# A graph layer and a small feed-forward layer: cell products in halves of a step, with a tile's product between them

## The chip, the cores and the metric

The kernel runs on one core of one Trainium2 chip. The metric is the time of one execution on the device in microseconds (us). The engines are TensorE (PE, whose weight loads the profile shows apart as PEld), VectorE (DVE), ScalarE (ACT), GpSimd (POOL) and SyncE (SP, which here only issues DMAs).

## What is computed

Inputs are `x` (8192 x 512), 131072 edges `(src, dst, edge_weight)`, a 512 x 512 weight and the weights of a seven-layer network of width 160. Cut to what matters:

```python
h   = layernorm(x) @ gnn_weight.T                     # 8192 x 512
x1  = x + segment_sum(edge_weight[:, None] * h[dst], src, 8192)
out = x1 + ffn(layernorm(x1))                         # ffn reads and writes a few columns of each row
```

For each edge a row of `h` (512 float32 numbers, 2 KB) has to be fetched by `dst`, scaled, and added to row `src`. The edges come in no order, so the kernel sorts them on the chip by the block of 128 rows that `src` lies in. There are 64 such blocks.

## The kernel before

**Heads.** The generator `project` makes `h` block by block (layer norm, transposes at L213, products at L238) and writes it to memory. Beside it the first part of the sort runs: `order(0)`.

**Sort.** `order` works on chunks of edges. A chunk (`chunk`, L328) compares the edges' blocks with the block numbers (DVE, L334), counts places with 8 products into `p_base` (L342) and 8 into `p_rank` (L357), and then puts each edge's packed address and weight into its cell by one-hot products into `p_c` (L402). These are the *cell products*. A chunk has four *quarters* (`c0` = 0, 2, 4, 6; in the code a loop in steps of SUB = 2), and each quarter has 16 values of `k` with 2 products each: 32 products. A quarter needs two operands, `blocks` (ACT, L375) and `put` (DVE, L376 and twice L384). They are made by `prepare`, which is called two quarters ahead, right behind the products of a quarter, and writes into the buffers that this quarter has just read (two buffers each). At the chunk's end ACT copies `p_c` out (L407). Seven chunks are in the first part and nine in the second. After its chunks each part runs `squeeze`, a long row of DVE operations.

**Gathered tiles.** A tile is 128 edges of one block. POOL fetches their rows with one indirect DMA (L570, 256 KB). DVE makes a one-hot matrix `hot` with the weights (L583, 28 tiles ahead). PE multiplies the two into the block's sum `p_g` (L881). Four tiles share a buffer `g`, and there are six such buffers, so POOL can be up to 24 tiles ahead of PE; a small product at L877 leads each buffer. `begin` goes through the 384 tiles of the first part, `evenly` through the 704 of the second, there with the feed-forward layers between.

**What sets the order.** PE, DVE, ACT and SP run in the order in which the program is written. The sort is a chain of generators. `chunk` yields `(tiles, blocks)`: how many gathered tiles, or head blocks, are to pass before its next step. The first part runs beside `project` and goes by `blocks`. Of the second part, `order(1)` with `fine` = 1, the first 24 steps run beside `project`, which takes them to just ahead of the first cell products; 16 more steps run straight behind it (L614), which is the rest of its first chunk and 6 steps into its second; and what is left, some eight chunks, runs beside the gathered tiles of `begin`, one step whenever the tile number `t` reaches `due` (L907). `due` grows by what each step yields; for a chunk that is 33 tiles in all. In `begin` the cell products of the four quarters stand behind tiles 0, 4, 8 and 9 of this part of a chunk.

In the profile one product of float32 is two MATMULs and two weight loads. A quarter therefore shows as 64 MATMULs of L402, a gathered tile as 2 of L881.

Of the kernel before, what the change touches and what calls it, by code (L numbers as in the profile page):

```python
# [34 lines left out]
def tile_gnn_ffn(  # L35
# [35 lines left out]
    GC, GQ, CAP, SUB = 8, 8, 40, 2  # L71
# [251 lines left out]
    def cut(n, size, fine):  # L323

        parts = -(-n // size) if fine else 1
        return [slice(n * i // parts, n * (i + 1) // parts) for i in range(parts)]

    def chunk(ck, ps_c, q, col, fine):  # L328


        hot = ck.tile([P, GC, NB, GQ], BF16, name="hot")
        for cs in cut(GC, 2, fine):
            n = cs.stop - cs.start
            nc.vector.tensor_tensor(  # L334
                hot[:, cs], each.rearrange("p (o b) g -> p o b g", o=1).to_broadcast([P, n, NB, GQ]),
                blk[:, q, cs].rearrange("p c (o g) -> p c o g", o=1).to_broadcast([P, n, NB, GQ]),
                OP.is_equal)
            yield 1, cs.stop // GC

        p_base = ps_c.tile([P, NB, GQ], F32, name="p_base")  # L340
        for c in range(GC):
            nc.tensor.matmul(p_base, above, hot[:, c], start=(c == 0), stop=(c == GC - 1))  # L342
        cum = ck.tile([P, GC, NB, GQ], BF16, name="cum")
        nc.scalar.copy(cum[:, 0], p_base)  # L344
        yield 2, 0
        for c in range(1, GC):
            nc.vector.tensor_tensor(cum[:, c], cum[:, c - 1], hot[:, c - 1], OP.add)  # L347
            if c % 2:
                yield 1, 0
        for cs in cut(GC, 2, fine):  # L350
            nc.vector.tensor_tensor(cum[:, cs], cum[:, cs], hot[:, cs], OP.mult)
            yield 1, 0
        yield 0, 2
        p_rank = ps_c.tile([P, GC, NB // GC, GQ], F32, name="p_rank")
        nb = NB // GC
        for i in range(GC):
            nc.tensor.matmul(p_rank, eye, cum[:, :, i * nb : (i + 1) * nb, :], start=(i == 0),  # L357
                             stop=(i == GC - 1))
        yield 2, 0
        rank = ck.tile([P, GC, GQ], F32, name="rank")  # L360
        nc.vector.tensor_reduce(rank, p_rank.rearrange("p c b g -> p c g b"), AX.X, OP.add)
        slot = ck.tile([P, CG, 1], BF16, name="slot")
        nc.vector.tensor_tensor(slot[:, :, 0], rank.rearrange("p c g -> p (c g)"), par, OP.add)
        yield 1, 0
        at = ck.tile([P, CG, 2, HALF], BF16, name="at")
        ready = {}

        def prepare(c0):

            if c0 >= GC:  # L370
                return
            n = SUB * GQ
            cs = slice(c0 * GQ, c0 * GQ + n)
            blocks = ck.tile([P, SUB, GQ, NB], F32, name="blocks", bufs=2)
            nc.scalar.copy(blocks, hot[:, c0 : c0 + SUB].rearrange("p c b g -> p c g b"))  # L375
            nc.vector.tensor_tensor(  # L376
                at[:, cs].rearrange("p n h s -> p n (h s)"),
                lots.rearrange("p (o h) s -> p o (h s)", o=1).to_broadcast([P, n, CAP]),
                slot[:, cs].to_broadcast([P, n, CAP]), OP.is_equal)
            yield 1, 0  # L380
            put = ck.tile([P, n, 2, 2, HALF], F32, name="put", bufs=2)
            for i, val in enumerate((val_a, val_w)):
                v = val[:, q, c0 : c0 + SUB, :].rearrange("p c (g a b) -> p (c g) a b", a=1, b=1)
                nc.vector.tensor_tensor(put[:, :, :, i, :], at[:, cs],  # L384
                                        v.to_broadcast([P, n, 2, HALF]), OP.mult)
                yield 1, 0
            ready[c0] = blocks, put

        yield from prepare(0)
        yield 0, 1  # L390
        yield from prepare(SUB)
        p_c = ps_c.tile([P, GQ, 2, HALF], F32, name="p_c")
        yield 0, 1
        nc.tensor.matmul(p_c.rearrange("p g w s -> p (g w s)"), nil[:, :P], nil, start=True,
                         stop=False)
        for c0 in range(0, GC, SUB):
            blocks, put = ready.pop(c0)
            for k in range(SUB * GQ):
                c, g = divmod(k, GQ)
                last = c0 + SUB == GC and k == SUB * GQ - 1  # L400
                for h in range(2):
                    nc.tensor.matmul(p_c[h * NB : (h + 1) * NB, g], blocks[:, c, g, :], put[:, k, h],  # L402
                                     start=False, stop=last)
            yield from prepare(c0 + 2 * SUB)
            yield 1, c0 // SUB % 2 if c0 + SUB < GC else 0
        for i, cells in enumerate((cells_a, cells_w)):
            nc.scalar.copy(cells[:, col : col + GQ * HALF].rearrange("p (g s) -> p g s", s=HALF),  # L407
                           p_c[:, :, i, :])
# [128 lines left out]
    def order(part):  # L537

        qs, col, fine = (range(QA), 0, 0) if part == 0 else (range(QA, NQ), CARRY, 1)
        with tc.tile_pool(name="ck", bufs=1) as ck, \  # L540
                tc.tile_pool(name="ps_c", bufs=1, space=PSUM) as ps_c:
            for q in qs:
                for tiles, blocks in chunk(ck, ps_c, q, col, fine):
                    yield tiles * PACE[0], blocks
                col += GQ * HALF
        with tc.tile_pool(name="sq", bufs=1) as sq, \
                tc.tile_pool(name="ps_q", bufs=2, space=PSUM) as ps_q:
            for tiles, blocks in squeeze(part, sq, ps_q, fine):
                yield tiles * PACE[1], blocks
# [45 lines left out]
    LEAD, BEGUN = 2, 24  # L595
# [15 lines left out]
        if b == NB // 2:  # L611
            x_0 = load_x(0)
    assert first is None
    for n in range(BEGUN + 16):  # L614
        if n >= begun:
            next(second)
    for t in range(early, AHEAD * GS):
# [543 lines left out]
```

## Time and profile before

| | |
|---|---|
| median of 3 runs (lowest to highest) | 2087.0 us (2076.41 to 2090.85) |
| the profiled execution: its time, its span | 2088.5 us, 2086.7 us |
| mean granted TensorE clock | 0.915 |

Busy time in us by stage, from windows of the profiled execution:

| stage (us from the start) | length | PE | DVE | ACT | POOL | DMA share | clock |
|---|---|---|---|---|---|---|---|
| heads, first part of the sort (0 to 367) | 367 | 344.6 | 260.8 | 201.6 | 22.1 | 0.32 | 0.99 |
| first gathers, rest of a chunk (367 to 412) | 45 | 20.0 | 11.2 | 6.9 | 23.5 | 0.58 | 0.62 |
| tiles with eight chunks between (412 to 843) | 431 | 379.0 | 236.1 | 77.1 | 274.3 | 0.68 | 0.92 |
| tiles with the squeeze (843 to 885) | 42 | 37.3 | 41.7 | 4.5 | 34.4 | 0.70 | 1.00 |
| the rest, most of it tiles with the layers (885 to 2086.7) | 1201.7 | 971.2 | 439.5 | 99.0 | 759.4 | 0.67 | 0.90 |

Busy times are from the first start to the last end of an engine's instructions, without its gaps. A MATMUL's end is modelled, so starts are more to be trusted than ends. "Issue" in these views is time in which an engine waited for nothing that the profile shows. A granted clock below 1 means that PE was held at a lower rate for part of the stretch.

### The profile page before, as it was taken

What the parts mean: (1) busy time and instruction counts of PE and PEld (TensorE: products, weight loads), DVE (VectorE), ACT (ScalarE), POOL (GpSimd) and SP (SyncE); (2) the same over time, 40 slices, a digit from 0 to 9 for tenths busy, and PEclk for the clock granted to TensorE, in tenths of its full rate; (3) what the DMA queues carried; (4) which work ended last, traced back from release to release, by engine and by line L of the source; (5) the groups of instructions that cost most, each with busy time, mean ns of one, the idle gap of its engine ahead of it and who ended that gap; (6) DMA issues with size and microseconds to landing.
All of it is one profiled execution on the core that took longest, in us unless ns stands there. A gap on an engine that the chain in (4) does not pass through costs nothing.

```text
span 2086.7 us, 24158 instructions
## 1 busy us (share of the span) xinstructions
PE 1752.0 (84%) x9317; PEld 841.0 (40%) x9317; DVE 989.3 (47%) x2520; ACT 389.1 (19%) x521; POOL 1113.7 (53%) x1138
## 2 busy tenths in 40 slices
PE   7999989598888988874987698897988969697878
PEld 4555544344444444322332243342433334243444
DVE  6676788365455554983322324233332434234322
ACT  5565644211211111110000010100101001010111
POOL 4000000466666666787666666666666666666550
PEclk9999999699998999988998898998989989898989
DMA  5233322567676676677786667686686857757561
GB/s 174 82 102 102 102 91 87 147 198 216 207 215 205 202 229 212 204 233 232 238 273 181 189 177 262 182 268 184 182 266 181 269 173 212 224 168 245 165 180 47
DMA packets 140923, 391.37 MB, mean 188 GB/s; under 512 B 20352, under 2 KB 21376, under 8 KB 140800
## 3 DMA queue, kind: packets, MB, share of 16 engines
q0 software_dynamic: 87952, 286.45, 45.8%
q1 hardware_dynamic: 52048, 101.72, 14.3%
q8 instruction: 76, 1.25, 0.2%
q10 hardware_dynamic: 800, 1.57, 0.2%
q14 instruction: 47, 0.39, 0.1%
HBM read 339.33 MB, written 50.33 MB: 187 GB/s over the span
## 4 chain that ended last, share of the span: by engine, by line
PE 62%; issue 11%; DVE 9%; another core or an unknown queue 9%; POOL 5%; DMA 2%; ACT 1%; DVEq 0%; POOLq 0%; ACTq 0%
PE p_g L881 34%; PE p_g L238 8%; PE p_c L402 7%; POOL g L570 5%; DVE hot L583 2%; PE p_a L666 2%; PE p_a L668 2%; DMA g<-h_rows,at_dst 2%; PE p_base L342 1%; PE p_rank L357 1%; PE p_g L213 1%; PE p_j L877 1%; PE p_b L660 1%; DVE ln L714 1%
## 5 line engine op out<-in xcount | busy, mean ns | idle before, releaser
L570 POOL DMA_INDIRECT g<-h_rows,at_dst x1088 | 1091.6, 1003 | 915.9 <-issue 646.8
L881 PE MATMUL p_g<-g,hot 128*128 128x512 f32 x2176 | 1099.1, 641 | 38.5 <-issue 38.4
L881 PEld LDWEIGHTS p_g<-g,hot 128*128 128x128 f32 x2176 | 408.0, 201 | 434.0 <-issue 423.8
L583 DVE TENSOR_SCALAR hot<-lanes,at_row,at_w 128x128 f32<-128x128 f32 x1088 | 324.9, 354 | 238.2 <-remote 111.7
L238 PE MATMUL p_g<-xg,g 128*128 128x512 f32 x512 | 237.7, 608 | 2.9 <-ACT g L215 2.9
L402 PE MATMUL p_c<-put,blocks 128*64 128x40 f32 x4096 | 163.4, 235 | 72.1 <-issue 70.5
L402 PEld LDWEIGHTS p_c<-put,blocks 128*64 128x64 f32 x4096 | 145.7, 144 | 116.1 <-issue 108.3
L375 ACT CAST blocks<-hot 128x1024 f32<-128x1024 bf16 x64 | 131.2, 2077 | 255.3 <-issue 212.0
L640 DVE TENSOR_SCALAR hb<-p_b,b_b 128x128 f32<-128x128 f32 (+1 forms) x54 | 18.1, 336 | 257.1 <-PE p_b L660 93.3
L238 PEld LDWEIGHTS p_g<-xg,g 128*128 128x128 f32 x512 | 94.8, 195 | 99.9 <-issue 95.7
L877 PEld LDWEIGHTS <-hot 128*1 128x1 bf16 x272 | 21.5, 79 | 238.8 <-issue 209.3
L384 DVE TENSOR_TENSOR put<-at,val_a 128x640 f32<-128x640 bf16 x64 | 52.8, 824 | 119.1 <-remote 75.7
L347 DVE TENSOR_TENSOR cum<-cum,hot 128x512 bf16<-128x512 bf16 x112 | 47.6, 425 | 87.9 <-ACT cum L344 72.4
L877 PE MATMUL p_j<-g,hot 128*1 128x4 bf16 x272 | 45.7, 168 | 49.5 <-issue 25.3
L643 ACT ACTIVATE ha<-p_a,b_a 128x512 f32<-128x512 f32 (+1 forms) x54 | 34.6, 640 | 243.7 <-remote 103.1
L171 ACT ACTIVATE rstd_f<-mv_f,eps 128x8 f32<-128x8 f32 (+1 forms) x9 | 2.7, 300 | 395.1 <-DVE st L863 220.2
L936 DVE TENSOR_TENSOR xu<-xu,p_g 128x512 f32<-128x512 f32 x64 | 43.7, 682 | 61.1 <-PE p_g L881 23.1
L770 ACT COPY back<-p_v 128x256 f32<-128x256 f32 (+1 forms) x9 | 3.3, 371 | 358.8 <-PE p_a L652 177.1
L891 DVE TENSOR_TENSOR xg<-xg,p_g 128x512 f32<-128x512 f32 x64 | 43.6, 682 | 55.4 <-PE p_g L881 53.3
L668 PEld LDWEIGHTS p_a<-hb,w_z 128*128 128x128 f32 x360 | 49.7, 200 | 18.4 <-issue 17.9
L213 PE MATMUL p_g<-ident,g 128*128 128x128 f32 x256 | 40.3, 282 | 19.5 <-ACT g L204 13.4
L376 DVE TENSOR_TENSOR at<-lots,slot 128x640 bf16<-128x640 bf16 x64 | 52.4, 819 | 0.3
(182 smaller groups left out, 1152.0 us busy)
## 6 DMA issues: line engine op xcount, KB each, us to landing
g<-h_rows,at_dst POOLq DMA_INDIRECT x1088
xg<-in_x_dram SPq DMA_DIRECT2D x16, 1024.0 KB
x_rows<-xg SPq DMA_DIRECT2D x32, 512.0 KB
xu<-x_rows SPq DMA_DIRECT2D x16, 1024.0 KB
g<-in_x_dram SPq DMA_DIRECT2D x31, 512.0 KB
h_rows<-g SPq DMA_DIRECT2D x31, 512.0 KB
out_dram<-xu SPq DMA_DIRECT2D x7, 2048.0 KB
xg<-in_gnn_wT_dram ACTq DMA_DIRECT2D x1, 1024.0 KB
```

The source lines that it names most:

```text
L213: nc.tensor.transpose(p_t[:, k * P : (k + 1) * P], t[:, 2 + b % 2, k * P : (k + 1) * P], ident)
L238: nc.tensor.matmul(p_h, t[:, b % 2, k * P : (k + 1) * P], gw[:, k, :], start=(k == 0), stop=(k == KD - 1))
L347: nc.vector.tensor_tensor(cum[:, c], cum[:, c - 1], hot[:, c - 1], OP.add)
L375: nc.scalar.copy(blocks, hot[:, c0 : c0 + SUB].rearrange("p c b g -> p c g b"))
L376: nc.vector.tensor_tensor(at[:, cs].rearrange("p n h s -> p n (h s)"), lots.rearrange("p (o h) s -> p o (h s)", o=1).to_broadcast([P, n, C ...
L384: nc.vector.tensor_tensor(put[:, :, :, i, :], at[:, cs], v.to_broadcast([P, n, 2, HALF]), OP.mult)
L402: nc.tensor.matmul(p_c[h * NB : (h + 1) * NB, g], blocks[:, c, g, :], put[:, k, h], start=False, stop=last)
L570: nc.gpsimd.indirect_dma_start(out=g[:, k, :], out_offset=None, in_=h_rows, in_offset=bass.IndirectOffsetOnAxis(ap=at_dst[part][:, i : i + ...
L583: nc.vector.tensor_scalar(hots[n][:, k, :], lanes, at_row[part][:, i : i + 1], at_w[part][:, i : i + 1], op0=OP.is_equal, op1=OP.mult)
L668: nc.tensor.matmul(p_a[:, g, :], w_z[:, i, g, :], last_hb, start=False, stop=((g + 1) * T % 512 == 0 or g == NG - 1))
L877: nc.tensor.matmul(p_j[:, part, :], hot[:, GS - 1, :].bitcast(BF16)[:, 1:2], g.rearrange("p k d -> p (k d)").bitcast(BF16).rearrange("p (k ...
L881: nc.tensor.matmul(p_g, hot[:, i, :], g[:, i, :], start=(k == 0), stop=(k == TILES[part] - 1))
```

## The change

Where `fine` is set (the second part), `chunk` yields once more within each quarter, after 8 of its 16 values of `k`, with half a tile; the yield at the quarter's end goes from one tile to half a tile, so that a chunk's sum stays 33. The count of steps that run straight behind `project` goes from 16 to 20, since one chunk's cell products are among them and now have four more yields.

```diff
                 for h in range(2):
                     nc.tensor.matmul(p_c[h * NB : (h + 1) * NB, g], blocks[:, c, g, :], put[:, k, h],
                                      start=False, stop=last)
+                if fine and k == SUB * GQ // 2 - 1:
+                    yield 0.5, 0
             yield from prepare(c0 + 2 * SUB)
-            yield 1, c0 // SUB % 2 if c0 + SUB < GC else 0
+            yield 1 - 0.5 * fine, c0 // SUB % 2 if c0 + SUB < GC else 0
...
-    for n in range(BEGUN + 16):
+    for n in range(BEGUN + 20):
         if n >= begun:
             next(second)
```

## The prediction

> **What bounds the kernel now.** I began with the page's costliest groups, to see how much of the change's own work there is.
>
> ```profile
> L570 POOL DMA_INDIRECT g<-h_rows,at_dst x1088 | 1091.6, 1003 | 915.9 <-issue 646.8
> L881 PE MATMUL p_g<-g,hot 128*128 128x512 f32 x2176 | 1099.1, 641 | 38.5 <-issue 38.4
> L402 PE MATMUL p_c<-put,blocks 128*64 128x40 f32 x4096 | 163.4, 235 | 72.1 <-issue 70.5
> ```
>
> The cell products keep PE for 163 us and have 72 us of idle time before them that no visible wait explains. Second, the waits of the stage in which the change acts, 412 to 843 us:
>
> ```profile
> POOL g L570 <- PE p_g L881: 89.5, 25, 14.8
> PEld p_c L402 <- issue: 76.3, 112, 1.9
> ...
> PE p_c L402 <- issue: 46.8, 83, 1.7
> ```
>
> POOL waits 89.5 us in 25 pieces for a buffer that PE has not freed, so PE sets the pace here; and PE loses time to "issue" inside the cell products. Third, the timeline of PE shows where in a run of products it is lost. This is the first quarter of one chunk; columns are start, length, line, count, idle time before.
>
> ```profile
> 481.85 1.59 PE L402 MATMUL p_c<-put,blocks 128*64 128x40 f32 x46
> 483.72 0.33 PE L402 MATMUL p_c<-put,blocks 128*64 128x40 f32 x5 [0.28 <-issue]
> ...
> 486.57 0.33 PE L402 MATMUL p_c<-put,blocks 128*64 128x40 f32 x4 [1.08 <-issue]
> 487.30 0.23 PE L402 MATMUL p_c<-put,blocks 128*64 128x40 f32 x1 [0.39 <-issue]
> ...
> 503.34 2.06 PE L402 MATMUL p_c<-put,blocks 128*64 128x40 f32 x64
> 505.33 1.12 PE L881 MATMUL p_g<-g,hot 128*128 128x512 f32 x2
> 506.39 2.08 PE L402 MATMUL p_c<-put,blocks 128*64 128x40 f32 x64
> ```
>
> I call a MATMUL with its weight load a pair: a tile is 2, a quarter 64. 46 pairs run at 31 ns, and then pairs come by ones and fives at steps of 0.72 us. A full quarter at speed takes 2.0 us (503.34); this one takes 7.6, to the next line's start at 489.44. Fourth, windows tell what goes with it (PE, PEld, DVE, ACT, POOL busy, clock, DMA share, GB/s):
>
> ```profile
> 47.70:51.56 3.86, 3.86 (x130) 3.81 (x129) 2.82 (x6) 3.43 (x5) 0.00 (x0) 1.00 0.24 90
> 371.00:401.00 30.00, 9.36 (x106) 6.99 (x103) 7.26 (x11) 2.39 (x2) 22.99 (x24) 0.61 0.73 212
> 404.70:408.39 3.69, 3.69 (x67) 3.60 (x66) 0.00 (x0) 0.00 (x0) 0.00 (x0) 0.50 0.00 0
> ```
>
> Beside the heads 128 pairs pass without a gap. While 24 gathers move 212 GB/s, only 106 pass in 30 us; when the traffic is gone, 66 pass without a gap again, even at half the clock. So PE can take some 46 pairs from a store, and while gathers move the store is refilled slowly. I count 7 pairs per us from the mild stalls (5 per 0.72 us) and 2.6 per us from the long ones (28 pairs in 10.8 us from 652.0). Fifth, POOL's timeline at the end of the same stall:
>
> ```profile
> 488.39 0.94 POOL L570 DMA_INDIRECT g<-h_rows,at_dst  x1 [0.30 <-issue]
> 489.64 0.95 POOL L570 DMA_INDIRECT g<-h_rows,at_dst  x1 [0.30 <-issue]
> 493.28 0.95 POOL L570 DMA_INDIRECT g<-h_rows,at_dst  x1 [2.69 <-PE p_g L881]
> ```
>
> Gathers come every 1.25 us until the six buffers are full; then POOL waits and PE is quick. A long stall ends when POOL has caught up. Between chunks' quarters PE takes a tile in 0.93 us (four in 3.73), quicker than POOL's 1.25, so POOL starts the cell products 15 or 16 tiles ahead, not 24, and has 8 or 9 gathers to catch up.
>
> From the starts in that timeline, the 32 quarters of the stage last 139.2 us: first quarters 40.4, second 52.9, third 23.2, fourth 22.8. At 2.0 each they would be 64. The loss is 75 us: seven long ones (over 7 us each, all in first or second quarters) lose 52.3, eighteen of 2.4 to 4.1 us lose 22.9, seven lose nothing.
>
> **The change, part by part.** *What moves.* Counting `due`: halves stand behind tiles 0 and 1, 4 and 5, 8 and 9, 9 and 10. The half-tile yields add up so that the third quarter's second half and the fourth's first half come behind the same tile, 9, as one run of 64 pairs. A chunk thus has runs of 32, 32, 32, 32, 32, 64, 32 pairs in place of four of 64. `prepare` moves one tile later for the third and fourth quarters' operands; it issues one ACT cast (2.08 us) and three DVE operations (0.82 us each) and no DMA. In DVE's queue the `put` waits for PE to leave the old buffer, as now, and behind it stand `hot`s, made 28 tiles ahead, and the adds of finished blocks. For the fourth quarter, from the end of its buffer's last reader to its first product there will be three tiles, two halves and a tile: 2.8 + 2.0 + 1.1 = 5.9 us. In the trace, from 499.41 the cast ended at 501.63 and the last `put` at 501.34, so 2.2 us are needed. I cost this at 0; uncovered, it would be up to 2 us per chunk, 16 in all. The 20 steps for 16 put the stream ahead of `begin` at the same place: 0. The chunk's sum of 33 is unchanged, so the squeeze comes behind the same tiles: 0.
>
> *Mild stalls.* 46 pairs run free and 18 at 7 per us: 2.6 us. Put a tile of 0.93 us between: 6.5 pairs come in and 2 go, so 4.5 fewer are short, 0.65 us saved. Seven of the eighteen are in first and second quarters: 4.6 us. Third and fourth quarters now have one tile in 128 pairs and will have two, with a run of 64 still there: 0.65 us in each of eight chunks, 5.2. Together -10. Bounds: 0, and all 22.9.
>
> *Long stalls.* Here I walked the first half of a chunk by hand: a store of 46, refill at 2.6 pairs per us, 8 gathers owed (10.0 us), a buffer freed every fourth tile, and traffic that ends 3 us after the last gather (the first 24 gathers end at 401.2, PE is quick from 404.7). Now: 50 pairs in 1.5 us, 14 more at the low rate (6.9); four tiles (10.6); the freed buffer keeps gathers going to 15.6 and traffic to 18.6; the second quarter gets 21 pairs by then and 43 quick ones (19.9); four tiles (23.6). Changed: half (1.0), tile (2.0), 18 pairs and 14 at the low rate (7.9); three tiles (10.7) and the freed buffer: traffic to 18.7; the half gets 21 pairs by then and 11 quick ones (19.0); tile (20.0), half from the refilled store (21.0), three tiles (23.8). The same, because the end of the traffic, not the length of the run, ends the stall. I take 0. Bounds: a third of 52.3 gained (17), or 30 lost (the second rival).
>
> *Changes between kinds.* The tile at 505.33 between two quarters takes 1.06 us to the next line's start; one in a row takes (3.73 - 0.10)/4 = 0.91. So 0.15 us for going in and out, three more times in each of eight chunks: +4. Bounds 2 to 8.
>
> Sum: -10 + 0 + 4 = -6 us against the profiled 2088.5, whose span of 2086.7 has 1.8 us around it. It carries to the end: counted in the timeline, POOL is 20 tiles ahead of PE at 842 us and 6 ahead at 885, and from there sets the pace, so what PE wins by freeing buffers sooner, POOL has as well. The profiled execution lies 1.5 us above the median of 2087.0, so I say 2081.
>
> The Trainium skill, in "Runtime: NRT & Kernel Launch", section on instruction fetch mechanics, says that an engine's instructions come in blocks of 16 KiB and that fetching them is hidden, since they are issued more slowly than they are filled in. The trace has 76 such packets of 16 KiB, but not the hiding. By that rule there would be no short supply, the split could save nothing, and the sum would be +4. The page "TensorE: Matmul & The Clock Gate" (table at its head) gives PE a queue of 64 instructions, 32 pairs: a half would just fit, a quarter would not. The trace's 46 pairs is more than that.
>
> **The rivals.** *The stalls go* (faster). A half of 32 pairs is below 46, so each half might run free. For it: of the eight first quarters, which come after some 20 tiles without such products, two run through, five stop between pairs 44 and 58, and only one at 23. Against it: the second half comes after one tile, with the store at 14 and some. If the mild ones go and a third of the long: -22.9 - 17.4 + 4 = -36, 2051. All: 2016.
>
> *Traffic starts again between the halves* (slower). The tile between may be the fourth of a buffer. It then frees it, POOL sends four more gathers (5 us), and the second half meets both an empty store and new traffic. Tiles 1, 5 and 9 share their place in the buffer, and a chunk of 33 moves that place by one, so it is two chunks in eight, three halves each: 6 x 5 = 30 us, less 6: 2111. It decides if these halves lose over 4.5 us each; against it, the gathers so gained are not owed later.
>
> *It does not do what it says* (no change). The stall hangs on the gathers owed and not on the run, nothing shortens, and only the +4 stays: 2091.
>
> **How the numbers follow.** Forecast 0.40, no effect 0.17: both within 1% (2066 to 2108), which is about what a measurement of this kernel can tell from no change. Stalls go 0.22, traffic again 0.21. The term bounds give 2088.5 - 23 - 17 + 2 to 2088.5 + 30 + 8, less 1.5: 2049 to 2125. The far ends need all terms at once, so the range is 2050 to 2118; within the likeliest case 2070 to 2095.
>
> **What would show it.** Right: L402 in runs of 32 and one of 64; the stage from 412 shorter by some 6 us; first and second quarters still with a few stalls over 5 us, ending when POOL goes idle; POOL's wait for `p_g` near 85 us. The faster rival: L402's idle "issue" below half of 46.8 and POOL's wait below 60. The slower: long stalls in second halves behind a freed buffer. I am wrong on the store if a half stops before pair 30 after a quiet stretch, and wrong on the cover of `prepare` if PE waits for `put` or `blocks`.

## The result, and the profile after

| | median of 20 runs (lowest to highest) |
|---|---|
| before | 2083.2 us (2070.0 to 2092.4) |
| changed | 2090.1 us (2083.4 to 2104.2) |
| ratio | 1.0044, 95% interval 1.0026 to 1.0061 |

The change costs 5 to 13 us where 6 were to be gained. That is within the 1% band and inside the range, but on the other side of the forecast. The profiled execution took 2089.6 us, its span is 2087.7 us and its mean granted clock 0.912. Below the edit the line numbers grow by two: L570, L877 and L881 are L572, L879 and L883 now.

The costliest groups of the changed kernel, the three that were shown of before:

```profile
L572 POOL DMA_INDIRECT g<-h_rows,at_dst x1088 | 1095.0, 1006 | 905.9 <-issue 648.0
L883 PE MATMUL p_g<-g,hot 128*128 128x512 f32 x2176 | 1108.0, 642 | 43.8 <-issue 41.7
L402 PE MATMUL p_c<-put,blocks 128*64 128x40 f32 x4096 | 163.8, 236 | 62.3 <-issue 60.5
```

Its waits from 412 to 843 us (us in total, times, longest; POOL waits for a free buffer, the other two lines are stops inside the cell products):

```profile
POOL g L572 <- PE p_g L883: 88.5, 26, 14.2
PEld p_c L402 <- issue: 87.4, 114, 1.9
...
PE p_c L402 <- issue: 37.1, 64, 1.8
```

The idle time before the cell products is 10 us less in this profile, 62.3 for 72.1, the size that was forecast. But the tiles (L883) show 9 us more busy time and 5 us more idle time, and POOL waits as long as before. What the products gained, the tiles gave back. PE's clock is at half rate in some stretches, as the next rows show, so a tile's busy time is not a constant; this turns out to be a part of the answer.

Next, the timeline of PE in the last of the eight chunks, changed kernel (start, length, line, count, idle time before):

```profile
804.03 1.13 PE L402 MATMUL p_c<-put,blocks 128*64 128x40 f32 x32
...
806.24 1.13 PE L402 MATMUL p_c<-put,blocks 128*64 128x40 f32 x32
807.30 2.84 PE L883 MATMUL p_g<-g,hot 128*128 128x512 f32 x6
810.08 1.13 PE L402 MATMUL p_c<-put,blocks 128*64 128x40 f32 x32
...
812.29 0.54 PE L402 MATMUL p_c<-put,blocks 128*64 128x40 f32 x8
813.25 0.29 PE L402 MATMUL p_c<-put,blocks 128*64 128x40 f32 x3 [0.42 <-issue]
...
823.22 0.23 PE L402 MATMUL p_c<-put,blocks 128*64 128x40 f32 x1 [1.18 <-issue]
823.38 5.49 PE L883 MATMUL p_g<-g,hot 128*128 128x512 f32 x6
```

A half is 32 of a quarter's 64 pairs. Three halves run free at 1.06 us each. The fourth stops after 8 pairs and lasts 11.1 us, to 823.38. Then three tiles take 5.49 us, where the three at 807.30 took 2.84: the clock has fallen to half (granted 0.50 from 815.80 to 828.80). Before, the second quarter of the same chunk lost its time in the same way. It was then at half clock too (0.50 from 824.96 to 827.48), but only for a run of 44 pairs without a gap; the four tiles behind it took 4.04 us, near the 3.70 of full speed:

```profile
819.38 0.78 PE L402 MATMUL p_c<-put,blocks 128*64 128x40 f32 x9
820.68 0.31 PE L402 MATMUL p_c<-put,blocks 128*64 128x40 f32 x3 [0.52 <-issue]
...
824.23 0.32 PE L402 MATMUL p_c<-put,blocks 128*64 128x40 f32 x3 [1.21 <-issue]
824.96 2.59 PE L402 MATMUL p_c<-put,blocks 128*64 128x40 f32 x44 [0.41 <-issue]
827.48 0.17 PE L877 MATMUL p_j<-g,hot 128*1 128x4 bf16 x1
827.58 4.04 PE L881 MATMUL p_g<-g,hot 128*128 128x512 f32 x8
```

POOL's timeline there, changed kernel, shows the price:

```profile
820.28 0.95 POOL L572 DMA_INDIRECT g<-h_rows,at_dst  x1 [0.30 <-issue]
829.14 0.95 POOL L572 DMA_INDIRECT g<-h_rows,at_dst  x1 [7.91 <-PE p_g L883]
...
839.90 1.03 POOL L572 DMA_INDIRECT g<-h_rows,at_dst  x1 [6.06 <-PE p_g L883]
```

POOL has filled all six buffers at 820.28 and then waits 7.91 us for PE: for the rest of the long stop, and for the three tiles at half clock that must pass until the next buffer is free. Before, the gathers ran on until 835.65 with no wait over 2.2 us, and only then came one of 5.85:

```profile
825.33 1.31 POOL L570 DMA_INDIRECT g<-h_rows,at_dst  x1 [2.14 <-remote]
...
835.65 0.95 POOL L570 DMA_INDIRECT g<-h_rows,at_dst  x1 [0.30 <-issue]
842.45 1.45 POOL L570 DMA_INDIRECT g<-h_rows,at_dst  x1 [5.85 <-PE p_g L881]
```

Counted by gathers, the changed kernel is 9.2 us ahead of the kernel before at the 276th, 2.8 at the 277th (the one behind the wait of 7.91 us), 1.9 at the 289th and 1.2 at the 384th. So it had gained in the chunks ahead, lost most of that here, and did not win it back in the next hundred gathers. The squeeze follows, and behind it POOL sets the pace. What is left at the end can't be read from this one pair: at the last gather the change is 6.5 us ahead, and it still ends 1.0 us later, because from its last gathered product to the end it takes 39.6 us for 32.0 before. The last section shows that this comes with either kernel.

### The profile page after: what moved, and what is told of

Its sections match the earlier page's. It is cut to its first block, busy times and chain, and to the rows that moved or that the text cites. A ratio compares the mean times of both kernels' runs of the same rounds, so it can differ in the third digit from the quotient of the medians.

```text
span 2087.7 us, 24157 instructions
## 1 busy us (share of the span) xinstructions
PE 1763.5 (84%) x9317; PEld 842.9 (40%) x9317; DVE 987.5 (47%) x2520; ACT 389.2 (19%) x521; POOL 1117.4 (54%) x1138
## 4 chain that ended last, share of the span: by engine, by line
PE 55%; issue 12%; POOL 10%; another core or an unknown queue 10%; DVE 9%; DMA 2%; ACT 1%; POOLq 0%; DVEq 0%; ACTq 0%
PE p_g L883 29%; POOL g L572 10%; PE p_g L238 8%; PE p_c L402 6%; DVE hot L585 2%; PE p_a L668 2%; PE p_a L670 2%; DMA g<-h_rows,at_dst 2%; PE p_rank L357 1%; PE p_base L342 1%; PE p_g L213 1%; PE p_b L662 1%; PE p_j L879 1%; DVE ln L716 1%
## 5 line engine op out<-in xcount | busy, mean ns | idle before, releaser
L572 POOL DMA_INDIRECT g<-h_rows,at_dst x1088 | 1095.0, 1006 | 905.9 <-issue 648.0
L883 PE MATMUL p_g<-g,hot 128*128 128x512 f32 x2176 | 1108.0, 642 | 43.8 <-issue 41.7
L883 PEld LDWEIGHTS p_g<-g,hot 128*128 128x128 f32 x2176 | 405.6, 200 | 436.8 <-issue 425.1
L402 PE MATMUL p_c<-put,blocks 128*64 128x40 f32 x4096 | 163.8, 236 | 62.3 <-issue 60.5
L402 PEld LDWEIGHTS p_c<-put,blocks 128*64 128x64 f32 x4096 | 144.8, 144 | 125.9 <-issue 119.5
L879 PEld LDWEIGHTS <-hot 128*1 128x1 bf16 x272 | 21.6, 79 | 250.7 <-issue 220.4
L879 PE MATMUL p_j<-g,hot 128*1 128x4 bf16 x272 | 45.7, 168 | 69.5 <-issue 36.2
L670 PEld LDWEIGHTS p_a<-hb,w_z 128*128 128x128 f32 x360 | 53.4, 213 | 18.2 <-issue 17.0
L670 PE MATMUL p_a<-hb,w_z 128*128 128x128 f32 (+1 forms) x360 | 52.7, 295 | 0.0
```

The source lines that it names most:

```text
L572: nc.gpsimd.indirect_dma_start(out=g[:, k, :], out_offset=None, in_=h_rows, in_offset=bass.IndirectOffsetOnAxis(ap=at_dst[part][:, i : i + ...
L670: nc.tensor.matmul(p_a[:, g, :], w_z[:, i, g, :], last_hb, start=False, stop=((g + 1) * T % 512 == 0 or g == NG - 1))
L879: nc.tensor.matmul(p_j[:, part, :], hot[:, GS - 1, :].bitcast(BF16)[:, 1:2], g.rearrange("p k d -> p (k d)").bitcast(BF16).rearrange("p (k ...
L883: nc.tensor.matmul(p_g, hot[:, i, :], g[:, i, :], start=(k == 0), stop=(k == TILES[part] - 1))
```

## The experiments

All ratios are against the kernel before on the same chip, with 12 runs of each kernel tried. A run is named below by the start of its label (h1 for h1_change_third). In each, the count of steps straight behind `project` is set so that the stream stands at the same place when the tiles begin.

**First set.** Prepare alone (products unsplit, a plain yield of half a tile ahead of `prepare`; shown against the kernel before), and halves in two quarters alone (shown against the change).

```diff
+            if fine:
+                yield 0.5, 0
             yield from prepare(c0 + 2 * SUB)
-            yield 1, c0 // SUB % 2 if c0 + SUB < GC else 0
+            yield 1 - 0.5 * fine, c0 // SUB % 2 if c0 + SUB < GC else 0
```
```diff
-                if fine and k == SUB * GQ // 2 - 1:
+                if fine and c0 < 2 * SUB and k == SUB * GQ // 2 - 1:
                     yield 0.5, 0
             yield from prepare(c0 + 2 * SUB)
-            yield 1 - 0.5 * fine, c0 // SUB % 2 if c0 + SUB < GC else 0
+            yield 1 - 0.5 * (fine and c0 < 2 * SUB), c0 // SUB % 2 if c0 + SUB < GC else 0
```

The control is the kernel before itself, and the second run the change.

> The kernel before, unchanged, timed against itself: the ratio should have 1.000 in its interval, and its width says what the other ratios can tell. Its profile is a second draw of before: if the stage from 412 us to the last cell products ends within 2 us of the first draw's 839, stage times can be compared between single profiles; if it differs by 5 us or more, as the two kernels' profiles did in the middle of the stage, they can't.

Measured: 1846.4 us, 0.9994 [0.9975, 1.0013].

> The changed kernel once more, on the chip that runs the other three. If its 7 us are in the kernel, the ratio is 1.002 to 1.006 again; if they were of the chip or the hour, it is 1.000. Its profile is a second draw: the loss inside runs of cell products (75 us before, 66 in the first draw of the change by the same count against 2.0 us per 64 pairs) should be below 75 again if the split really shortens stalls.

Measured: 1853.3 us, 1.0020 [1.0001, 1.0038].

> Only prepare moves one tile later; the 64 products of a quarter stay in one piece behind tiles 0, 4, 8 and 9. Theory A (the pieces cost: 24 more goings in and out at about 0.2 us): as before, ratio 1.000. Theory B (the operands for the next quarters come later, and the products or DVE's queue wait for them): as the change, 1.003 to 1.005. Theory C (nothing in this stage; what comes after it turns out otherwise): either.

Measured: 1844.7 us, 0.9998 [0.9983, 1.0014].

> Only the first and second quarters are halved (16 goings in and out more, prepare one tile later for both); third and fourth are whole behind tiles 8 and 9, as before. Theory A: two thirds of the change, 1.002 to 1.003. Theory B: all of it, 1.003 to 1.005, since only these two quarters are followed by a prepare. If the harm is in the joined run of 64 between tiles 9 and 10 and the half behind tile 10, it is gone: 1.000.

Measured: 1845.0 us, 0.9985 [0.9966, 1.0003].

The kernel before takes 1848 us on this chip, not 2083. The page of the control shows where the difference lies:

```profile
L570 POOL DMA_INDIRECT g<-h_rows,at_dst x1088 | 1095.2, 1007 | 678.8 <-issue 634.4
L402 PE MATMUL p_c<-put,blocks 128*64 128x40 f32 x4096 | 132.3, 232 | 3.0 <-DVE put L384 3.0
```

POOL's idle time is 237 us less, and beside "issue" it waits 44 us in all, for 269 in the profile before. The cell products have no idle time of "issue" here. The stops that the change is about do not happen on this chip, so these runs could not tell what they cost. What they show is the change without them: 0 to 7 us more, and nothing for prepare's later place.

**Second set**, on a chip where the products do stop. The change again; the halves with the *first* half of each quarter a tile earlier, so that the second half and `prepare` stand where the whole quarter stood before; and both kernels with PE kept at work in the last tens of us (`busy(4)` behind the products of `p_v`), since profiles of the same kernel differed there.

```diff
-        yield 1, 0
+        yield 1 - fine, 0
         at = ck.tile([P, CG, 2, HALF], BF16, name="at")
...
-                    yield 0.5, 0
+                    yield 1, 0
             yield from prepare(c0 + 2 * SUB)
-            yield 1 - 0.5 * fine, c0 // SUB % 2 if c0 + SUB < GC else 0
+            yield 1 - fine, c0 // SUB % 2 if c0 + SUB < GC else 0
+        if fine:
+            yield 1, 0
```
```diff
+        busy(4)
         v = fp.tile([P, T], F32, name="v", bufs=1)
```

> The changed kernel a third time. If the runs before took near 2085 us here (PE runs short while gathers move, as in the first profiles): 1.004 again if the loss belongs to that state of the chip. If they took near 1847 us (no such shortage, POOL never waits): 1.002 or less, and if the last 40 us are drawn by chance, as likely 1.000. The tail from the last gathered product to the end, 39 us in both profiles of the change and 31.5 in the four others, is 39 again if the change makes it so, and one or the other if it is chance.

Measured: 2093.5 us, 1.0051 [1.0027, 1.0075].

> The quarters are in halves, but the first half comes one tile sooner instead of the second one tile later, so that prepare keeps its place. Theory A (the pieces cost): as the change, 1.002 to 1.004. Theory B (prepare's delay, or where the pieces fall): 1.000. Theory C (chance of the tail): 1.000 where the tail is short in as many runs as before's.

Measured: 2079.3 us, 0.9987 [0.9955, 1.0019].

> The kernel before, with four more idle products on PE in the last unit, behind the products into p_v, where PE has its longest gaps. If the tail of 39 us comes from a clock window that finds PE too little busy there, all runs now have the short tail: 2 to 3 us less in the median, spread smaller, ratio 0.998 to 0.999. If not, 1.000.

Measured: 2084.1 us, 0.9988 [0.9960, 1.0017].

> The changed kernel with the same four products. Theory C: the change costs nothing once the tail is fixed, so the ratio is that of f3. Theory A: 1.002 to 1.004 above f3's.

Measured: 2091.0 us, 1.0032 [1.0003, 1.0062].

The loss is there again, and it stays with PE kept at work in the last tens of us, so nothing points to the end of the kernel as its place (that these products steady the end in every execution is not shown; the spread did not shrink). Splitting as such is not its cause: the same halves, the first a tile earlier, show no loss clear of noise.

**Third set**, on another such chip: the halves in all chunks but the last, only in the last (`q == NQ - 1` in the two conditions), and the two parts of the first set again. The time behind each result is that from the start of tile 241 to the start of tile 274, the last chunk, in the run's one profile.

```diff
-                if fine and k == SUB * GQ // 2 - 1:
+                if fine and q < NQ - 1 and k == SUB * GQ // 2 - 1:
                     yield 0.5, 0
             yield from prepare(c0 + 2 * SUB)
-            yield 1 - 0.5 * fine, c0 // SUB % 2 if c0 + SUB < GC else 0
+            yield 1 - 0.5 * (fine and q < NQ - 1), c0 // SUB % 2 if c0 + SUB < GC else 0
```

> Halves in every chunk of the second part but the last. Theory L (the loss is in the last chunk: tiles 241 to 274 took 52.5 and 54.4 us before, 58.7, 61.8 and 58.0 with the halves, and the chunks ahead of it are even): near before, 1.000 to 1.001, and the last chunk takes 52 to 55 us. Theory P (each chunk pays a little for its pieces): seven eighths of the change, 1.004. Both hold only where PE runs short while gathers move (runs before near 2085 us); where they take near 1847 us, 1.000.

Measured: 2113.7 us, 1.0037 [1.0010, 1.0064]; 53.4 us from tile 241 to 274.

> Halves in the last chunk alone. Theory L: the whole loss, 1.003 to 1.005, last chunk 58 to 62 us. Theory P: an eighth, 1.000 to 1.001. Theory H (the last chunk is hit only through what the halves before it did to POOL's lead): 1.000 here and in g1, last chunk 52 to 55 us.

Measured: 2114.2 us, 1.0054 [1.0034, 1.0075]; 60.5 us.

> Only prepare one tile later, once more, since the run of e3 was on a chip where PE does not run short (1847 us before). Theory B (prepare's delay): 1.004 on a chip of 2085 us. Theories L and P, in which the pieces do it: 1.000.

Measured: 2099.5 us, 0.9965 [0.9933, 0.9996]; 60.6 us in its profile.

> First and second quarters halved, third and fourth whole behind tiles 8 and 9, again for the chip's sake. In the profiles of the change the last chunk's second quarter stalls for 9 to 11 us (before 5 to 8) and its last three runs take 7 to 9 us (before 6.3 to 6.4). If the first is what costs, half to all of the loss stays: 1.002 to 1.004. If it is the half behind tile 10 and the joined run, next to the squeeze, 1.000.

Measured: 2106.0 us, 1.0042 [1.0014, 1.0069]; 58.2 us.

The last chunk alone costs as much as the whole change did on the other chips, and halves in the first two quarters are enough for it. But the other seven seemed to cost too, and the two do not add up. Prepare alone does not cost, although its one profile (2111.7 us, 12 above its own median) shows the long last chunk too.

**Fourth set**, the square that settles the place: the seven chunks as changed or with the first half earlier, and the last chunk the same two ways, on one chip. The edit on the change, here for the last chunk alone; for the converse its condition is `q < NQ - 1`:

```diff
-        yield 1, 0
+        early_q = fine and q == NQ - 1
+        yield 1 - early_q, 0
...
-                    yield 0.5, 0
+                    yield 0.5 + 0.5 * early_q, 0
             yield from prepare(c0 + 2 * SUB)
-            yield 1 - 0.5 * fine, c0 // SUB % 2 if c0 + SUB < GC else 0
+            yield 1 - 0.5 * fine - 0.5 * early_q, c0 // SUB % 2 if c0 + SUB < GC else 0
+        if early_q:
+            yield 1, 0
```

> The changed kernel once more, as one corner of a square of four kernels on one chip: the first seven chunks beside gathers with the halves where the change puts them or with the first half a tile earlier, and the last chunk the same two ways. On a chip where the quarters' runs stop beside gathers (the time near 2085 to 2105 us): 1.0035 to 1.006 of the time before. From tile 241 to tile 274 some 58 to 62 us.

Measured: 2094.6 us, 1.0051 [1.0024, 1.0079]; 62.6 us from tile 241 to 274.

> As the change in the first seven chunks; in the last chunk the first half of each quarter stands a tile earlier, and the second half and prepare stand where the products stood before. Theory that the cost lies in the last chunk (tile 241 to 274 takes 6 us longer, and nothing behind it gives it back): 0.998 to 1.002, and 52 to 55 us from tile 241 to 274. Rival, that every chunk pays its share through products that end a tile later: 1.003 to 1.005, since seven of eight chunks still pay.

Measured: 2088.6 us, 1.0013 [0.9986, 1.0039]; 53.5 us.

> The converse: first halves a tile earlier in the first seven chunks, and the last chunk as the change has it. Theory of the last chunk: 1.002 to 1.005 (it should stand above the kernel with all first halves earlier by some 6 us), and 58 to 62 us from tile 241 to 274. Rival of every chunk's share: 0.999 to 1.001, since one of eight chunks pays.

Measured: 2092.8 us, 1.0040 [1.0010, 1.0069]; 62.2 us.

> All first halves a tile earlier, once more. By both theories it stands at 0.997 to 1.002 of the time before, with 52 to 55 us from tile 241 to 274. If it comes out above 1.003, the earlier reading, that the place of the last products decides and not the splitting, falls.

Measured: 2083.1 us, 1.0004 [0.9979, 1.0030]; 53.9 us.

From the runs' means, the last chunk's place costs 7.3 us (the mean of h1 less h2 and h3 less h4; 95% interval 3.5 to 11.0 by drawing the runs again), that of the other seven 2.6 us (-1.2 to 6.3). So the last chunk is where the loss clear of noise lies. The windows from tile 241 to the 289th gather say what differs there, first h1 and then h4 (length, then PE, PEld, DVE, ACT, POOL busy, clock, DMA share, GB/s):

```profile
800.90:859.10 58.20, 46.02 (x326) 23.43 (x325) 30.94 (x69) 6.13 (x5) 31.31 (x30) 0.82 0.56 170
```
```profile
805.40:855.70 50.30, 41.79 (x328) 21.35 (x327) 29.05 (x64) 6.16 (x5) 31.09 (x31) 0.93 0.65 197
```

The same work takes 8 us longer, at a clock of 0.82 for 0.93. The waits of POOL in the same two stretches:

```profile
POOL g L572 <- PE p_g L883: 19.0, 3, 7.5
```
```profile
POOL g L574 <- PE p_g L885: 9.8, 4, 5.0
```

POOL loses 9 us more in fewer, longer waits. And the timeline of PE in h4 shows the stop in another place: the second half of the *first* quarter. It lasts 6.9 us, where the stop in h1 lasts 11.2; the three tiles behind it are slow here too, and the next halves run free.

```profile
812.19 1.12 PE L885 MATMUL p_g<-g,hot 128*128 128x512 f32 x2
813.25 0.66 PE L402 MATMUL p_c<-put,blocks 128*64 128x40 f32 x14
...
819.91 0.30 PE L402 MATMUL p_c<-put,blocks 128*64 128x40 f32 x1 [0.51 <-issue]
820.14 0.17 PE L881 MATMUL p_j<-g,hot 128*1 128x4 bf16 x1
820.24 4.47 PE L885 MATMUL p_g<-g,hot 128*128 128x512 f32 x6
824.64 1.13 PE L402 MATMUL p_c<-put,blocks 128*64 128x40 f32 x32
```

**Fifth set.** What sets the long stop in the last chunk: that its first half stands just behind tile 247, the last of a buffer, or that the products end a tile later? Both kernels with the last chunk's products moved one tile on, the squeeze left in place. (The change is shown; before, the second edit has 1 for `1 - 0.5 * fine`.)

```diff
-        yield 1, 0
+        yield 1 + (q == NQ - 1), 0
...
-            yield 1 - 0.5 * fine, c0 // SUB % 2 if c0 + SUB < GC else 0
+            yield 1 - 0.5 * fine - (q == NQ - 1 and c0 + SUB == GC), c0 // SUB % 2 if c0 + SUB < GC else 0
```

> The changed kernel, but in the last chunk beside gathers everything from the cell products on stands one more tile later (the squeeze not), so that no tile that frees a buffer stands just ahead of the first half. Theory of the buffer's place (a buffer freed just ahead of the first half, three halves that run free, then one stop of 9 to 11 us while POOL is full): tile 241 to 274 falls back to 52 to 56 us, ratio 0.999 to 1.002. Rival, that products which end later cost: 59 to 66 us, ratio 1.004 to 1.007.

Measured: 1846.0 us, 1.0003 [0.9986, 1.0020].

> The kernel before, unsplit, but in the last chunk everything from the cell products on stands one tile later (the squeeze not): a quarter ends behind the same tile as in the change. Theory of the buffer's place: 52 to 56 us from tile 241 to 274, ratio 0.998 to 1.002. Rival, that the later end costs and not the split: 58 to 62 us, ratio 1.003 to 1.005.

Measured: 1848.1 us, 1.0005 [0.9986, 1.0024].

Inconclusive: before takes 1847 us on this chip, so it is again one where the products do not stop, and neither theory was put to the test.

## Why the prediction was wrong

The account is made from starts to next starts of PE, over all profiles of chips where the products stop. "Tiles" take in the small product that leads each buffer. The first row holds tiles 10 to 241, with seven chunks: three profiles with unsplit products there (before, f3, g2) against six as changed (after, f1, f4, g1, h1, h2). The second holds tiles 241 to 274, the last chunk: before, f3, g1 against after, f1, f4, g2, h1, h3. Mean us, before and changed in each cell, with the time at half clock in the last column; the chunk's other products make up the rest of the total:

| | total | cell products | tiles | at half clock |
|---|---|---|---|---|
| first seven chunks | 379.5, 381.8 | 119.3, 114.5 | 234.2, 241.2 | 62.6, 66.0 |
| last chunk | 53.4, 60.6 | 16.9, 21.3 | 35.7, 38.4 | 7.9, 18.8 |

Single profiles of the first row spread from 372 to 389 us, so its small sums carry little. Those of the second do not overlap: 52.5 to 54.4 and 58.0 to 62.6 (g3, with whole quarters and a later `prepare`, is in neither group and had 60.6). The two together are 2.3 + 7.2 = 9.5 us. The timed square gave 2.6 and 7.3, but against first halves a tile earlier, not against unsplit products, and for the first row such agreement is luck. Against the forecast of -6, the last chunk missed by 8 us (7.2 for an eighth of -6), and the seven chunks by some 7.5 (2.3 for -5.3); the second of these rests on profiles that spread more than that.

- *What moves*: right. L402 comes in runs of 32, with one of 64, and the chunk's place did not change.
- *Mild stalls, -10*: the mechanism is there, the size is off. The seven chunks' products gained 4.8 us, for seven eighths of 10, 8.8, forecast. First and second quarters hold the gap: in all eight chunks they last 88.9 us before (mean of before and f3) and 89.2 changed (after, f1, f4, h1), where 4.6 less were forecast. The stops did not go, they moved: the first quarters fell from 42.9 to 26.0 us, their first halves running free (8.5 us for eight), and the second quarters rose from 46.0 to 63.2, most of it in their second halves. The sign for a wrong store, a half that stops before pair 30 after a quiet stretch, did not come in these four profiles, but it did with first halves a tile earlier (pairs 26 and 27 in f2, 23 in h3), so the 46 pairs are not a fixed size. Third and fourth quarters went from 48.2 to 45.3, for 5.2 forecast.
- *Changes between kinds, +4*: priced right for one change (tile at 805.19 to half at 806.24 us: 1.05), but not the whole effect on the tiles. They cost 7.0 us more in the seven chunks, of which 7 x 3 x 0.15 = 3.2 are changes. The term had no room for tiles behind a long stop at half clock, though the profile of before showed half clock, and 0.61 as the clock of a stretch of stops.
- *Long stalls, 0*: this is the step that failed. The walk through a chunk ended at the same us with whole quarters and with halves, because the end of the traffic and not the length of a run was to end a stall. For the first two quarters of all chunks together the products bear that out (88.9 and 89.2 us). But it was one chunk at one phase of the buffers, and it let the end of a stop be the end of its cost. In the last chunk three free halves bring nothing that lasts. From the start of tile 241, PE has passed tile 251, and freed its buffer, after 12.6 us in the change (810.1 less 797.5) and 14.0 before (819.4 less 805.4). The next buffer is free after 31.3 us in the change (828.8) and 26.1 before (831.5): the second quarter's stop of 11.1 us, for 8.1, stands a tile further on, and the tiles behind it run at half clock. In all six profiles with the change in this chunk, three halves take 1.1 us each and the fourth 9.0 to 11.4. In the means of the table, products +4.4 and tiles +2.7 are the 7 us, where the prediction had an eighth of -10 for the products, nothing of it for long stalls, and an eighth of +4 for the tiles.
- *It carries to the end*: borne out, and against the change. Moving the last chunk's halves changes the timed runs by 7.3 us and the stretch from tile 241 to 274 by some 8.7 (62.6 and 62.2 for 53.5 and 53.9). That it is POOL's pace behind the squeeze that keeps the loss is argued from its lead, 20 tiles at 842 us and 6 at 885 in both kernels, and not tested apart.
- *Prepare, 0*: right. PE waits for `put` or `blocks` at most 2.9 us in all beside the chunks in any profile of a chip with stops (7.6 in e4, on a chip without), and e3 and g3 (0.9998 and 0.9965) show no cost.
- *The rivals*: the faster one is out (37.1 us of "issue" in L402, not below 23.4; POOL's wait 88.5, not below 60). The slower one named the right place, second halves meeting traffic with an empty store behind a freed buffer, but not its rule: the buffer was freed ahead of a first half and not between the halves, its loss in seven chunks comes out small (2.6 us in the square with an interval that takes in 0, though g1 alone gave 1.0037), and its price was 7 us once and not 5 us six times. *It does not do what it says* comes nearest in time (2091), by luck: the stalls did change, by moving.

What stays open is why just that half of the last chunk meets the whole stop, and none does in the versions with first halves a tile earlier (their longest there is 6.9 us); the two runs that were to tell the buffer's place from the later end met a chip without stops. Nor do the traces say what PE waits for in a stop; "issue" is all they show. Open too is why moving `prepare` alone gave the long last chunk in one profile and no loss in the timed runs. No version beat the kernel before beyond doubt: the earlier first half came to 0.9987 and 1.0004, prepare alone to 0.9998 and 0.9965.

## What to carry to other kernels

A stop that comes from elsewhere, here while gathers move, need not be shortened by splitting the work that it hits: in this kernel the next piece met it (first quarters 16.9 us less, second 17.2 more), and the account has to include what the engine's clock does behind a longer stop. When a gain in one stage is fed to a helper engine with a few buffers, look at the last place ahead of the stage where that helper sets the pace: here only the loss there was clear of noise in the square. And compare several profiles before summing small terms: the same stretch spread by 17 us here, while the last chunk's piece was steady to 5.

## What was not expected of the hardware

- The same kernel before takes 1848 and 1847 us on two chips and 2083 to 2103 on the others. On the first two, most quarters' 64 pairs take 2.0 us beside the gathers too, and L402's idle time is 3.0 us for 72.1; what differs in the chips, no run shows.
- The section of the Trainium skill that the prediction weighed, "Runtime: NRT & Kernel Launch" on instruction fetch mechanics, calls the cost of fetching the next block mostly hidden. The traces do not speak against it: in all six profiles with the change in the last chunk, a 16 KiB packet of the instruction queue ends 1 to 3 us ahead of the long stop, and no other of 16 KiB moves until the stop is over (in the changed kernel one ends at 810.19 us and the next starts at 833.34). So the prediction's store that is refilled slowly describes the pairs that pass, but no packet of instructions is seen to be late in this stop.
- From the last gathered product to the end the same work takes 31 to 32 or 39 to 40 us, whatever the kernel. The windows of that stretch, first of h1 and then of h4 (columns as above), show it to be the clock:

```profile
2060.60:2091.70 31.10, 21.05 (x212) 13.54 (x210) 9.47 (x41) 6.31 (x12) 0.00 (x0) 0.93 0.12 38
```
```profile
2056.10:2095.20 39.10, 29.90 (x212) 20.07 (x210) 9.47 (x41) 6.31 (x12) 0.00 (x0) 0.63 0.09 30
```

The first is the change and the second the version that loses nothing, so a single profile's time can be 8 us off from this alone. The profile of the change has half clock there for 31.5 us in one piece. Its other stretches at half clock come in multiples of 3.4 us and begin at other places in each execution. The Trainium skill, "TensorE: Matmul & The Clock Gate", Part 1, has the clock decided in windows of 3413 ns that run free of the kernel's start, which agrees with these pieces and would leave the end of a run to chance.
